# Down projection by two levels of Strassen's scheme in an S4-gated feed-forward kernel on one Trainium2 core

## The chip, the cores and the metric

The kernel runs on one core of one Trainium2 chip. A core has five engines with queues of their own: TensorE (PE; its weight loads are shown apart as PEld), VectorE (DVE), ScalarE (ACT), GpSimd (POOL) and SyncE (SP), which here only issues DMAs. TensorE writes to PSUM, which is split into eight banks of 128 partitions by 512 f32 numbers; the program names the banks x0, x1, w0, w1, y0, y1, aux0 and aux1. Everything is f32. The metric is the device time of one execution in microseconds; the median of several runs is compared. The lower, the better.

## The reference

The input u has 2 x 1024 rows of 512 numbers. The rows are normalised; a state-space model (S4) convolves each row causally along its 512 numbers; a gated feed-forward network with low-rank additions to each of its three weights gives a gate. Cut to what matters:

```python
xn = layernorm(u)                                   # along the last axis, 512
K  = s4_kernel(Lambda, p, q, B, Ct, step, 512)      # one convolution kernel for all rows
s  = causal_conv(xn, K) + D * xn                    # written with rfft/irfft of length 1024
h1 = lora_linear(xn, w1, A1, B1)                    # x @ w.T + 2 * (x @ a.T) @ b.T, 512 -> 1376
h3 = lora_linear(xn, w3, A3, B3)
f  = lora_linear(silu(h1) * h3, w2, A2, B2)         # 1376 -> 512
out = u + s * silu(f)
```

## The kernel before

The 2048 rows are four blocks of 512 tokens (TB); blocks 0 and 1 form half `sb` = 0, blocks 2 and 3 half 1. The first part of the program loads the rows, normalises and transposes them (channels on partitions) and adds the low-rank products to the weights in place (`merge`, DVE, out of PSUM).

**Up projections.** The hidden axis has ten chunks of 128 and a last one of 96 (`HID` 1376). The ten are handled as five pairs (`NPAIR`), each by two levels of Strassen's scheme in Winograd's form: an outer one over weight and token halves, with sums on DVE (`outer_weight_sums`, `inner_weight_sum`, `outer_token_sum`, `inner_token_sum`), and an inner one, so that a pair is seven chains (j = 1 to 7) of seven products (i = 1 to 7) of 128 x 128 by 128 x 512. Class `Chain` issues them: ACT copies PSUM to SBUF between products, DVE adds a snapshot to PSUM (`total`, line 780) and combines (`plus`, line 870), POOL does the combinations whose inputs are both in SBUF, ACT the SiLU and POOL the product (`Gate`, line 837), which SP stores to `g_dram` (`store_g`).

The order on every engine is written out by hand: `at(place, what)` puts a step into a heap, and the loop that pops it emits the instructions in order of place. A place is one product; chain n of pair c begins at place 7 (2 + 7c + n), and `PLACES` says where its seven products stand after that. Engines take their own queue in that order and wait by semaphores; a product waits for its bank, so a late DVE or ACT step holds up PE. The last pair begins at place `t0` = 210 and its last product stands at 265. Between these places stand the loading and merging of the down weight (`load_w2`, `merge_down`), the down projection's weight sums (`second_weights`, line 1221) and the first loads of the gates (`load_g`).

**Down projection.** Eight units of 128 tokens of two blocks (256 rows each) run one after another (the first four two by two). A unit is one level of the scheme: seven products, each summed over five chunk pairs, and four of them over the last chunk too, of 128 x 128 by 128 x 256 (function `unit`, lines 1316 to 1415; the matmuls are line 756 in `product`). The sums over the gates are made on DVE for two units at a time (`group_piece`, line 1179). The S4 kernel is made meanwhile, some steps at a time (`s4_resolvent`, `s4_roots`, `s4_matrix`, lines 554 to 747): vector steps on DVE and a few matmuls, with a result of five 128 x 128 blocks in the tile `conv`. Because the convolution can't start before that, the first four units set their gates aside in DRAM (`o_dram`), and each of the last four takes one back (`hold`, `take_back`) beside its own.

**Convolution and end.** `conv_product` (line 930 for its matmuls) makes the convolution of 128 rows by a Toeplitz matrix in 128 x 128 blocks: eight matmuls of 128 columns with sums of the transposed tokens (`block_sums`, DVE). `result` adds the shared part (line 1310, DVE), multiplies by the gate (line 1312, DVE), adds the row (line 1313, POOL) and stores it.

Of the kernel before, what the change touches and what calls it, by code (L numbers as in the profile page):

```python
# [12 lines left out]
F32 = mybir.dt.float32  # L13
# [4 lines left out]
P = 128  # L18
# [51 lines left out]
def exp_neg(nc, pool, x, times):  # L70

    magic = 1.5 * 2.0**23
    n = pool.tile([P, 1], F32, tag="ex_n", name="ex_n")
    nx = pool.tile([P, 1], F32, tag="ex_x", name="ex_x")
    r = pool.tile([P, 1], F32, tag="ex_r", name="ex_r")
    p = pool.tile([P, 1], F32, tag="ex_p", name="ex_p")
    two_n = pool.tile([P, 1], I32, tag="ex_2n", name="ex_2n")
# [16 lines left out]
    for k in range(6, -1, -1):  # L94
        nc.vector.tensor_scalar(p, p, r, 1.0 / math.factorial(k), ALU.mult, ALU.add)
        yield
    nc.vector.tensor_scalar(two_n, n, 127.0, 2.0**23, ALU.add, ALU.mult)
    yield
    out = pool.tile([P, 1], F32, tag="ex_out", name="ex_out")
    nc.vector.scalar_tensor_tensor(  # L100
        out, p, times, two_n.bitcast(F32), ALU.mult, ALU.mult
    )
# [5 lines left out]
def s4_gated_ffn(  # L108
# [70 lines left out]
    g_dram = dram.tile([NSB * NJ, P, NHC, 2, JW], F32, name="g_dram")  # L179

    b12_dram = dram.tile([P, NSB, 2, TB], F32, name="b12_dram")
    i12_dram = dram.tile([P, 3, TB], F32, name="i12_dram")

    UNITS, HOLD = 2 * NSB * NJ, NSB * NJ
    o_dram = dram.tile([HOLD, 2, P, DIM], F32, name="o_dram")
# [8 lines left out]
    xr = xpool.tile([P, 3, NSB, 2, TB], F32, name="xr")  # L194
    tin = ctx.enter_context(ExitStack())
# [5 lines left out]
    xt = upool.tile([P, 4, NSB, 2, TB], F32, name="xt")  # L201
# [128 lines left out]
    def spill():  # L330
        for sb in range(NSB):
            nc.sync.dma_start(out=b12_dram[:, sb], in_=b12[sb])
        nc.sync.dma_start(out=i12_dram, in_=xr[:, :, 1, 0, :])
# [165 lines left out]

    def load_w2_factors():  # L500
        lora_tiles(0)
        for g in range(4):
            load_lora(nc.sync, g, b2T, a2, 3 * P * g, min(3 * P * (g + 1), HID))
# [14 lines left out]
    def merge_down(i):  # L518

        made = []  # L520
        groups = [g for g in range(4) if i + 3 * g < NHC]
        ps = [bank("y", True), bank("w", True), *(aux() for _ in groups[2:])]
        for g, to in zip(groups, ps):
            lo = (i + 3 * g) * P
            fc = CHUNK_AT.index(lo)
            rows = P if fc < LAST else LASTR
            d, h = lora_factors(g, lo, rows)
            to = to[:rows, :]
            nc.tensor.matmul(to, lhsT=h, rhs=d, start=True, stop=True)  # L529
            made.append((w2_chunk(fc), to))  # L530
        for m, when in zip(made, (1.15, 2.3, 4.3, 4.4) if i < 2 else (1.15, 1.9, 2.6)):
            after(when, lambda m=m: merge(*m))
# [4 lines left out]
    def s4_tile(shape, name):  # L537
        return work.tile(shape, F32, name=name, bufs=1)

    def s4_loads():  # L540
        par = s4["par"] = s4_tile([P, 10], "par")
        nc.sync.dma_start(out=par, in_=s4_par)
        vc = s4["vc"] = s4_tile([NST, 2, 2, NST], "vc")
        for half in range(2):
            nc.sync.dma_start(out=vc[:, :, half, :], in_=vcT)
        bp_sb = s4["bp"] = s4_tile([NST, 1], "bp_sb")
        nc.sync.dma_start(out=bp_sb, in_=bp)
        hcol = s4["hcol"] = s4_tile([P, 4, NDC], "hcol")
        nc.sync.dma_start(out=hcol, in_=half_col)
        s4["trig"] = s4_room().rearrange("p (a l) -> p a l", a=3)  # L550
        nc.sync.dma_start(
            out=s4["trig"][:, :2].rearrange("p a l -> p (a l)"),
            in_=half_row.to_broadcast([P, 2 * DIM]),
        )
# [5 lines left out]
    def s4_room():  # L560
        return room["w"][:, 5 * DIM :]

    def s4_resolvent():
# [3 lines left out]
        par, trig = s4["par"], s4["trig"]  # L567
        cos, sin, im = (trig[:, i, :] for i in range(3))
        lam_r, lam_i = par[:, 0:1], par[:, 1:2]
        two_over_step = yield from exp_neg(nc, work, par[:, 8:9], 2.0)  # L570
        den = const.tile([P, DIM], F32, tag="lo_d", name="den")
# [16 lines left out]
        res = den  # L588
        nc.vector.tensor_tensor(res[:NST, :], re[:NST, :], den[:NST, :], mult)
        yield  # L590
        nc.vector.tensor_tensor(res[NST:, :], im[NST:, :], den[NST:, :], mult)
        yield


        pb = aux()
        for c in range(2):
            nc.tensor.matmul(
                pb[:, c : c + 1],
                lhsT=s4["vc"][:, c, :, :].rearrange("m h n -> m (h n)"),
                rhs=s4["bp"],  # L600
                start=True,
                stop=True,
            )
        yield from pause(3)
        y = s4_tile([P, 2, 2], "y")
        nc.vector.tensor_copy(y[:, :, 0], pb[:, 0:2])
        yield
        nc.vector.tensor_copy(y[:, :, 1], par[:, 6:8])
        yield

        v = s4_tile([P, 2, 2, 2], "v4")
        tmp = s4_tile([P, 2], "vtmp")
        for i in range(2):
            xr_, xi = par[:, 2 + 2 * i : 3 + 2 * i], par[:, 3 + 2 * i : 4 + 2 * i]
            nc.vector.tensor_scalar(tmp, y[:, 1, :], xi, None, mult)
            yield
            nc.vector.scalar_tensor_tensor(v[:, i, :, 0], y[:, 0, :], xr_, tmp, mult, add)
            yield
            nc.vector.tensor_scalar(tmp, y[:, 0, :], xi, None, mult)
            yield  # L620
            nc.vector.scalar_tensor_tensor(v[:, i, :, 1], y[:, 1, :], xr_, tmp, mult, sub)
            yield
        v4 = v.rearrange("p a b c -> p (a b) c")
        wv = s4_tile([P, 4, 2], "wv")
        nc.vector.tensor_copy(wv[:NST], v4[:NST])
        yield
        nc.vector.tensor_scalar(wv[NST:, :, 0], v4[NST:, :, 1], -1.0, None, mult)
        yield
        nc.vector.tensor_copy(wv[NST:, :, 1], v4[NST:, :, 0])
        yield  # L630
        s4["res"], s4["wv"] = res, wv
        yield from pause(8)

    def s4_roots():

        hcol = s4["hcol"]
        edft = s4["edft"] = s4_room().rearrange("p (a c j) -> p a c j", a=3, c=NDC)
        nc.sync.dma_start(out=edft[:, :2], in_=dft)
# [10 lines left out]
        k = s4_tile([P, NDC, 8], "k")  # L649
# [3 lines left out]
        cos, sin, cos_l, sin_l = (hcol[:, i, :] for i in range(4))  # L653

        def op(name, a, b, o):
            t = s4_tile([P, NDC], name)
            nc.vector.tensor_tensor(t, a, b, o)
            yield
            return t

        mul = mult
        dr = yield from op("dr", k11r, cos, mul)
        nc.vector.tensor_scalar(dr, dr, 1.0, None, add)
        yield
        di = yield from op("di", k11i, cos, mul)
        nr = yield from op("nr", k10r, cos, mul)
        ni = yield from op("ni", k10i, cos, mul)
        d2 = yield from op("d2", (yield from op("t0", dr, dr, mul)), (yield from op("t1", di, di, mul)), add)
        nc.vector.reciprocal(d2, d2)
        yield  # L670
        qr = yield from op("qr", (yield from op("t2", nr, dr, mul)), (yield from op("t3", ni, di, mul)), add)
        qi = yield from op("qi", (yield from op("t4", ni, dr, mul)), (yield from op("t5", nr, di, mul)), sub)
        nc.vector.tensor_tensor(qr, qr, d2, mul)
        yield
        nc.vector.tensor_tensor(qi, qi, d2, mul)
        yield
        mr = yield from op("mr", (yield from op("t6", k01r, qr, mul)), (yield from op("t7", k01i, qi, mul)), sub)
        mi = yield from op("mi", (yield from op("t8", k01r, qi, mul)), (yield from op("t9", k01i, qr, mul)), add)
        er = yield from op("er", k00r, mr, sub)
        ei = yield from op("ei", k00i, mi, sub)  # L680
        ar = yield from op("ar", (yield from op("u0", er, cos_l, mul)), (yield from op("u1", ei, sin_l, mul)), sub)
        ai = yield from op("ai", (yield from op("u2", er, sin_l, mul)), (yield from op("u3_", ei, cos_l, mul)), add)

        z = (edft[:, 2], room["zi"].rearrange("p (c j) -> p c j", c=NDC))
        for lc in range(NDC):
            e_r, e_i = edft[:, 0, lc, :], edft[:, 1, lc, :]
            a_r, a_i = ar[:, lc : lc + 1], ai[:, lc : lc + 1]
            for i, (f, g, o) in enumerate(((a_i, a_r, add), (a_r, a_i, sub))):
                tz = conv[:, DIM:]
                nc.vector.tensor_scalar(tz, e_i, f, None, mul)  # L690
                yield
                nc.vector.scalar_tensor_tensor(z[i][:, lc, :], e_r, g, tz, mul, o)
                yield
        s4["z"] = z
        yield from pause(8)

    def s4_matrix():
# [23 lines left out]
        f = s4["res"]  # L721
# [19 lines left out]
        k2s = s4["k2s"]  # L741
        both = conv[:, : 2 * P].rearrange("p (n t) -> p n t", n=2)
# [175 lines left out]

    def conv_product(lhs, x01, x12, sb, tok, tag):

# [391 lines left out]
    def unit(u, read, held=None, wait=False):  # L1316
# [8 lines left out]
        if u >= HOLD:  # L1325
            pl.load_in()
# [268 lines left out]
```

## Time and profile before

Three runs took 443.93, 442.70 and 442.58 us, median 442.7. The profiled execution has a span of 441.0 us from its first to its last instruction; the runs shown give no other time for that execution, so the median stands 1.7 us above the span.

| | busy, us | share of the span | instructions |
|---|---|---|---|
| PE | 434.3 | 98% | 1704 |
| PEld | 269.1 | 61% | 1704 |
| DVE | 317.6 | 72% | 536 |
| ACT | 144.3 | 33% | 296 |
| POOL | 207.9 | 47% | 156 |

An f32 matmul and its weight load are two records each in this table. DMA queues take 36.3% of sixteen engines' span and move 53.61 MB. The mean granted TensorE clock is 0.998. The first matmul of the down projection starts at 269.0 us of the span.

### The profile page before, as it was taken

How to read it: one execution, taken by the hardware profiler on the slowest of the kernel's cores; microseconds unless marked ns; L12 is line 12 of the kernel's file. 1: busy time of each engine (PE TensorE's matmuls, PEld its weight loads, DVE VectorE, ACT ScalarE, POOL GpSimd, SP SyncE). 2: the span in 40 equal slices, each digit the busy share in tenths (PEclk: the TensorE clock that was granted, in tenths of full speed). 3: DMA queues.
4: the chain of work that ended last, by engine and by line, in shares of the span. 5: the costliest groups of instructions: out<-in, count | busy, mean ns of one | idle time of the engine just before them, and what ended most of it. 6: DMA issues, size and time to landing. Idle time of an engine off the chain costs nothing.

```text
span 441.0 us, 5158 instructions
## 1 busy us (share of the span) xinstructions
PE 434.3 (98%) x1704; PEld 269.1 (61%) x1704; DVE 317.6 (72%) x536; ACT 144.3 (33%) x296; POOL 207.9 (47%) x156
## 2 busy tenths in 40 slices
PE   7999999999999999999999999999999999999996
PEld 7645334344444444444443446888898999999996
DVE  5899999954974687469745796979786885653234
ACT  2777242453255324532453242211101212212221
POOL 1416468895689368946894468400000122222221
PEclk9999999999999999999999999999999999999999
DMA  8931304025102500250035526395901832422211
GB/s 242 364 83 44 124 0 149 10 84 159 36 24 80 159 24 25 88 170 25 25 129 206 162 94 214 94 364 189 344 33 71 296 129 95 144 97 95 77 67 48
DMA packets 35467, 53.61 MB, mean 122 GB/s; under 512 B 4689, under 2 KB 21521, under 8 KB 35313
## 3 DMA queue, kind: packets, MB, share of 16 engines
q1 hardware_dynamic: 35088, 52.69, 36.3%
q10 hardware_dynamic: 352, 0.60, 0.4%
q8 instruction: 13, 0.21, 0.2%
q14 instruction: 14, 0.11, 0.1%
HBM read 33.88 MB, written 19.40 MB: 121 GB/s over the span
## 4 chain that ended last, share of the span: by engine, by line
PE 86%; DVE 7%; DMA 2%; ACT 2%; issue 1%; POOL 0%; SPq 0%; DVEq 0%; ACTq 0%; POOLq 0%
PE x L756 43%; PE y L756 22%; PE w L756 11%; PE aux L930 4%; PE w L930 2%; DMA s<-in_x_dram 1%; DVE xt L328 1%; DVE s L453 1%; DVE w L441 1%; DMA w<-in_w1T_dram 1%; PE y L529 1%; PE aux L711 1%; DVE t_in L343 1%; ACT c L254 1%; DVE aux L1310 1%
## 5 line engine op out<-in xcount | busy, mean ns | idle before, releaser
L1313 POOL TENSOR_TENSOR o<-o,xin 128x512 f32<-128x512 f32 (+1 forms) x17 | 23.3, 1369 | 133.0 <-DVE o L1312 133.0
L837 POOL TENSOR_TENSOR s<-c,s 128x512 f32<-128x512 f32 (+1 forms) x44 | 63.2, 1442 | 17.6 <-ACT c L829 12.4
L776 ACT COPY s<-x 128x512 f32<-128x512 f32 (+1 forms) x54 | 31.5, 584 | 84.5 <-PE x L756 84.4
L756 PE MATMUL x<-t_in,s 128*128 128x512 f32 (+1 forms) x148 | 55.4, 501 | 0.0
L870 POOL TENSOR_TENSOR s<-ua_three,s 128x512 f32<-128x512 f32 x20 | 35.9, 1793 | 25.4 <-DVE s L780 25.4
L780 DVE TENSOR_TENSOR s<-s,y 128x512 f32<-128x512 f32 (+1 forms) x54 | 36.0, 679 | 15.7 <-PE y L756 10.6
L756 PEld LDWEIGHTS x<-t_in,s 128*128 128x128 f32 x148 | 26.6, 190 | 23.3 <-issue 11.7
L870 POOL TENSOR_TENSOR ua_three<-ua_three,s 128x512 f32<-128x512 f32 x20 | 30.6, 1529 | 13.8 <-DVE s L780 13.8
L756 PE MATMUL y<-t_in,s 128*128 128x256 f32 (+1 forms) x108 | 35.9, 459 | 0.1
L1335 ACT COPY z<-x 128x256 f32<-128x256 f32 x24 | 8.8, 371 | 70.5 <-PE x L756 70.4
L870 POOL TENSOR_TENSOR s<-u_three,s 128x512 f32<-128x512 f32 x20 | 29.4, 1474 | 1.8 <-ACT c L829 1.0
L1310 DVE TENSOR_TENSOR aux<-aux,m 128x384 f32<-128x384 f32 x32 | 18.1, 565 | 15.8 <-PE aux L930 14.3
L829 ACT ACTIVATE c<-c 128x512 f32<-128x512 f32 x40 | 25.2, 632 | 12.9 <-DVE c L870 12.9
L756 PEld LDWEIGHTS y<-t_in,s 128*128 128x128 f32 x108 | 20.1, 190 | 11.6 <-issue 8.1
L794 ACT COPY w<-x 128x512 f32<-128x512 f32 (+1 forms) x37 | 21.1, 570 | 11.6 <-PE x L756 11.5
L870 POOL TENSOR_TENSOR u_three<-ua_three,u_three 128x512 f32<-128x512 f32 x10 | 15.6, 1556 | 13.4 <-DVE u_three L780 13.3
L756 PE MATMUL x<-t_in,w 128*128 128x512 f32 x40 | 21.0, 605 | 0.0
L756 PE MATMUL x<-xt,w 128*128 128x512 f32 x40 | 20.7, 598 | 0.0
L756 PE MATMUL x<-xr,w 128*128 128x512 f32 x40 | 20.6, 614 | 0.0
L756 PE MATMUL x<-xr,s 128*128 128x512 f32 x40 | 20.5, 614 | 0.0
L756 PE MATMUL x<-xt,s 128*128 128x512 f32 x40 | 20.4, 592 | 0.0
L756 PE MATMUL y<-xt,w 128*128 128x512 f32 x40 | 19.8, 592 | 0.0
(302 smaller groups left out, 908.7 us busy)
## 6 DMA issues: line engine op xcount, KB each, us to landing
g_dram<-s SPq DMA_DIRECT2D x40, 256.0 KB, 2.1
g<-g_dram SPq DMA_DIRECT2D x10, 512.0 KB, 5.8
xin<-in_x_dram SPq DMA_DIRECT2D x16, 256.0 KB, 2.7
out_dram<-o SPq DMA_DIRECT2D x14, 256.0 KB, 2.0
t_in<-g_dram SPq DMA_DIRECT2D x6, 512.0 KB, 4.1
w<-in_w1T_dram SPq DMA_DIRECT2D x10, 256.0 KB, 3.6
w<-in_w3T_dram SPq DMA_DIRECT2D x10, 256.0 KB, 4.9
t_in<-in_x_dram SPq DMA_DIRECT2D x8, 256.0 KB, 5.7
```

The lines of the kernel that those rows point to most:

```text
L254: nc.scalar.activation(value("c"), x_in[b][tt], AF.Copy, accum_out=sums_of_x[b][:, 0, tt : tt + 1])
L756: nc.tensor.matmul(ps[:, cols], lhsT=lhsT, rhs=rhs if parts == 1 else rhs[:, cols], start=first and i == 0 and part == 0, stop=i == len(pa ...
L776: nc.scalar.copy(t, self.x)
L780: nc.vector.tensor_tensor(t, t, self.y, add)
L794: nc.scalar.copy(self.w, self.x)
L829: nc.scalar.activation(c, c if src is None else src, AF.Silu)
L837: nc.gpsimd.tensor_tensor(g, act, g, mult)
L870: (nc.vector if o < 20 else nc.gpsimd).tensor_tensor(to, a, b, add)
L930: nc.tensor.matmul(to[:, n * P : (n + 1) * P], lhsT=x_, rhs=by, start=start, stop=True, skip_group_check=True,)
L1310: nc.vector.tensor_tensor(y[:, P:], y[:, P:], m[:, n * P : (n + 3) * P], add)
L1313: (nc.vector if last else nc.gpsimd).tensor_tensor(o, o, self.xin[h][:, cols], add)
L1335: nc.scalar.copy(t, xb)
```

## The change

The diff has some 1,300 lines. It does this:

- **Down projection in two levels.** Four units of 512 tokens (128 of each block) take the place of the eight. A unit has seven outer chains (j) of seven inner blocks (n); each block is a 128 x 128 by 128 x 128 product over two chunk pairs (eight chunks in all). The fifth pair of chunks and the last 96 rows go through the inner level alone, into the four outer chains of `EXTRA`. All of it is issued by `Unit.chain` and `down_product`.
- **Sums.** Weight: three more outer matrices on DVE and one in place (`weight_outer`), and seven inner sets (`weight_inner`). Gates: four outer sums of 1024 columns per unit, on POOL but for one (`g_outer`), and seven inner sets of four sums of 256 columns on DVE (`g_inner`), made ahead into a ring of nine places. The fifth pair: `rest_sums`, the first on DVE, the later ones on POOL.
- **Results.** Partial results stay in two banks of x, w or y; ACT takes snapshots; `combine` makes the four quarters of a gate on DVE out of four sources.
- **S4** runs between places 64 and 193 of the up projections; no gate is set aside in DRAM. The transposed tokens go to `x_dram` (`spill`) and come back unit by unit (`load_conv`) into places that the up projections have left; their convolution sums are on POOL (`conv_sums`).
- **Order.** After the up projections the places are microseconds: `pe(n, what)` advances a clock by n x 0.2236, and the other steps stand at fixed distances from it. It is an order of emission only.
- The chunks that load and merge the down weight are dealt to the row groups anew (`W2_AT`); `xt` lives on to the end.

Cut to its core:

```diff
-    UNITS, HOLD = 2 * NSB * NJ, NSB * NJ
-    o_dram = dram.tile([HOLD, 2, P, DIM], F32, name="o_dram")
+    UNITS = NTT
+    g_dram = dram.tile([UNITS, P, NHC, NSB, 2, P], F32, name="g_dram")
+    x_dram = dram.tile([UNITS, P, NDC, NSB, 2, P], F32, name="x_dram")
...
+    def inner_sums(eng, m, i, left, fifth=None):
+        m00, m10, m01, m11 = m
+        s2, s3, s4_ = i
+        s5 = m01 if fifth is None else fifth
+        if left:
+            todo = ((s3, m00, m01, sub), (s2, m11, s3, sub), (s5, m01, m11, add))
+        else:
+            todo = ((s3, m11, m01, sub), (s2, s3, m00, add), (s5, m01, m00, sub))
+        for to, a, b, op in (*todo, (s4_, m10, s2, sub)):
+            eng.tensor_tensor(to, a, b, op)
...
+    EXTRA = {2: (0, 0), 3: (0, 1), 7: (1, 1), 4: (1, 2)}
+    def down_product(u, j, n, to, plain=True, rest=True):
+        pairs = []
+        if plain:
+            a = inner_operand(*gi[u, j], True, n)
+            b = inner_operand(quarters(wm[j]), wi[j], False, n)
+            pairs += [(a[:, g], b[:, g]) for g in range(2)]
+        if rest and j in EXTRA:
+            ...
+        product(part(to, n), pairs, plain and j in (1, 7) and n in (1, 5))
...
+    steps(first, 64.1, 0.3, 33)
+    steps(first, 75, 1.5, 3)
+    steps(first, 118, 1.8, 12)
+    steps(s4_roots(), 142, 0.45, 80)
+    steps(s4_matrix(), 184, 0.3, 30)
+    at(t0 + 36, s4_shared)
+    at(t0 + 21.5, lambda: load_g(0))
+    for n, name in enumerate((5, 6)):
+        at(t0 + 30.5 + 3.2 * n, lambda name=name: g_outer(nc.gpsimd, 0, name))
+    at(t0 + 27, down_weights)
+    for n, name in enumerate((7, 6, 5, 4)):
+        at(t0 + 27.1 + 1.5 * n, lambda name=name: weight_outer(nc.vector, name))
+    for n, j in enumerate((1, 2)):
+        at(t0 + 37 + 4 * n, lambda j=j: weight_inner(nc.vector, j))
+    at(t0 + 42.5, lambda: g_inner(nc.vector, 0, 1, room["w"][:, 30 * P :]))
...
+    at(-0.5, lambda: load_rest(0))
+    at(0.2, lambda: g_inner(nc.vector, 0, 2, fifth[2]))
+    for when, j in ((0.5, 6), (3.7, 5), (6.9, 7), (10.1, 3), (17.5, 4)):
+        at(when, lambda j=j: weight_inner(nc.vector, j))
+        at(when + 1.5, lambda j=j: g_inner(nc.vector, 0, j, fifth.get(j)))
+    at(3, lambda: g_outer(nc.gpsimd, 0, 3))
+    at(4.5, lambda: g_outer(nc.vector, 0, 7))
+    for n in range(4):
+        at(11 + 1.5 * n, lambda: next(rw, None))
+    at(15, lambda: rest_sums(nc.vector, 0))
...
+        if h == 0:
+            at(clock[0] - (7.2, 10.4)[s], lambda: conv_sums(nc.gpsimd, u, s))
...
+        at(b[1] + 0.1, lambda: load_g(u))
+        if u == 1:
+            t5, t6, t3 = 16, 21.5, 24.5
+            whens = 28.5, 30, 36.5, 38.5, 41, 43, 45
+        for t, name in ((t5, 5), (t5 + 2.7, 7), (t6, 6), (t3, 3)):
+            at(t, lambda name=name: g_outer(nc.gpsimd, u, name))
+        for j, when in zip(order, whens):
+            at(when, lambda j=j: g_inner(nc.vector, u, j))
...
+    U = units[0]
+    for j in (1, 2, 6, 5, 7, 3):
+        U.chain(j, rest=j not in EXTRA)
+    for j in (2, 3, 7):
+        U.chain(j, plain=False)
+    conv_slot()
+    U.chain(4)
+    conv_slot()
+    ahead(U, 1)
+    for u in range(1, UNITS):
+        U, final = units[u], u == UNITS - 1
+        for j in FINAL if final else ORDER:
+            U.chain(j)
+            if j in ((6, 7, 4, 2) if final else (6, 3, 7, 4)):
+                conv_slot()
+            if final and j == 2:
+                conv_slot("y")
+        if not final:
+            ahead(U, u + 1)
```

`ORDER` is (1, 6, 5, 3, 2, 7, 4), `FINAL` (1, 6, 5, 7, 4, 2, 3). The very last convolution (`conv_last`) is issued column block by column block, ten matmuls in place of eight, so that its results can be finished one after another.

## The prediction

> **What bounds the kernel now.** I read the head of the page first, then busy time by stretches, then the chain that ended last in order of time, then the order of VectorE and GpSimd at the change of stage.
>
> ```profile
> PE 434.3 (98%) x1704; PEld 269.1 (61%) x1704; DVE 317.6 (72%) x536; ACT 144.3 (33%) x296; POOL 207.9 (47%) x156
> ...
> PE 86%; DVE 7%; DMA 2%; ACT 2%; issue 1%; POOL 0%; SPq 0%; DVEq 0%; ACTq 0%; POOLq 0%
> ```
>
> TensorE is busy 98% of the span and carries 86% of the chain. Stretches (start:end, length, then PE, PEld, DVE, ACT, POOL busy, clock, DMA share, GB/s):
>
> ```profile
> 180.00:210.00 30.00, 30.00 (x83) 12.68 (x83) 18.99 (x27) 10.92 (x20) 18.96 (x15) 1.00 0.31 95
> ...
> 252.00:257.00 5.00, 5.00 (x13) 2.12 (x12) 4.97 (x8) 1.88 (x4) 0.46 (x1) 1.00 0.30 97
> ...
> 272.00:277.00 5.00, 5.00 (x24) 4.37 (x24) 4.05 (x3) 0.00 (x0) 4.84 (x4) 1.00 0.27 92
> ```
>
> PE has no gap in the up projections, at the change of stage, or in the down projections, and the clock is full, so any product taken out shortens the run, as long as no wait comes in. The change of stage is the narrow place: DVE 4.97 of 5 at 252, POOL 4.84 of 5 at 272. In the chain (start, length, what) a matmul counts as two records, with its weight loads hidden:
>
> ```profile
> 310.58 1.03 PE aux L641 x8
> ...
> 328.13 2.68 PE aux L711 x24
> ...
> 370.60 1.12 PE aux L930 x10
> 371.71 2.16 PE x L756 x10
> ```
>
> So 128 columns take 1.12/5 = 0.224 us and 256 columns 2.16/5 = 0.432 us. The first down matmul starts at 269.00, the last ends at 437.25 (matmul records of the timeline): 168.25 us without a gap.
>
> **TensorE, removed and added.** Before: 8 units of 39 products of 256 columns (7 times 5 chunks, 4 for the last 96 rows) = 312 x 0.432 = 134.8, 16 convolution products of 8 matmuls = 128 x 0.224 = 28.7, S4 products 0.53 + 1.03 + 2.68 = 4.2; in all 167.7, against 168.25 measured. After: in each unit 7 chains of 7 blocks of 2 chunks (98), 28 for the fifth pair of chunks, 16 for the last rows, 32 for the convolutions = 174; four units and 2 more in the last convolution give 698 x 0.224 = 156.4. That is -11.9. The S4 products (4.2) move to the up projections, where PE is 30.00 of 30.00 busy, so they cost what they cost now. **Net -7.7.**
>
> [...]
>
> **S4's vector steps.** Some 30 us of DVE leave the down stage (284.9 to 335.6) for 64 to 193 places of the up order, with 7 to 13 us of idle DVE in each 30 us. They queue ahead of the chains' additions, which free PE's banks. One group, 4.6 us after the S4 matrix, lies among the outer weight sums of the last pair (199 to 206), where DVE runs without a pause. Bounds 0 to 3; I take 0.5, as the stretch has caught up by 206.45.
>
> **The end of the up projections.** Out: two weight sums of 1024 columns and three small ones (1.23 + 1.22 + 1.18 + 0.90 + 0.56 = 5.1 as measured). In, on DVE: four of 1024 (4 x 1.22), one of 256, and three inner sets of four of 256 at 0.34 from start to start (12 x 0.34): 9.3 us, of 23 between 246 and 269. On POOL two outer sums of 1024 (from 0.725 at 256 and 1.27 at 512 columns: estimate 2.36 each), which fall into its idle 5.8 us before 256.54, once load_g (on SP behind the gates' stores) has landed. The third weight set is queued ahead of the additions that release the y bank for the fourth chain's last product; in the trace that addition ends about 0.9 us before PE needs it. Without blocking DVE comes 1 to 2 us late; if every sum waits for a POOL operation, 5. Bounds 0 to 6; I take 1.
>
> **How DVE and POOL share.** A sum with both inputs in SBUF is stretched by a POOL operation, one that reads PSUM isn't (0.68 everywhere). Timeline, first DVE, then POOL (start, duration):
>
> ```profile
> 276.01 1.75 DVE L1179 TENSOR_TENSOR s<-room,s 128x512 f32<-128x512 f32 x1
> 277.68 2.28 DVE L1221 TENSOR_TENSOR w_a<-w_a 128x1024 f32<-128x1024 f32 x1
> 279.89 1.49 DVE L1221 TENSOR_TENSOR w_b<-w_b 128x256 f32<-128x256 f32 x1
> ...
> 277.17 1.71 POOL L870 TENSOR_TENSOR s<-ua_three,s 128x512 f32<-128x512 f32 x1
> 278.96 2.13 POOL L837 TENSOR_TENSOR s<-c,s 128x512 f32<-128x512 f32 x1
> ```
>
> Here they alternate strictly: the sum at 279.89 ends 0.29 after the POOL operation does. But elsewhere DVE keeps its turn:
>
> ```profile
> 48.53 1.28 DVE L328 TENSOR_TENSOR xt<-b,xr 128x512 f32<-128x512 f32 x2
> 49.73 1.28 DVE L328 TENSOR_TENSOR xt<-xr,xt 128x512 f32<-128x512 f32 x2
> 50.94 1.74 DVE L341 TENSOR_TENSOR t_in<-xr 128x1536 f32<-128x1536 f32 x1
> ...
> 48.69 5.12 POOL L870 TENSOR_TENSOR s<-ua_three,s 128x512 f32<-128x512 f32 x1 [6.04 <-DVE s L780]
> ```
>
> Five sums without a break ran undisturbed while POOL waited 4 us. [...]
>
> **The first unit.** PE runs six chains of 14 products (3.14 us each), so DVE must make two inner sets (8 x 0.34 = 2.7 us) per chain. By the third chain's third block (7.2 us after the start) ten sums must be done; they begin 0.65 after the last up product: 4.1 us if DVE keeps its turn, 3 us to spare. The next three chains need 24 sums and one of 1024, 9.3 us for 9.4 of PE; no slack is added there. If POOL's operations come between, 9 us late. The last gates, the load of the fifth pair and what stands behind it on SP also end here (second rival). Bounds 0 to 12; I take 2.5.
>
> **Units 1 to 3.** Per unit of 174 x 0.224 = 39.0 us, DVE: 28 inner sums (9.5), totals out of PSUM 2 x (0.57 + 0.68), combinations 4 x 1.2, convolution additions 8 x 0.58, products with the gate 4 x 0.61: 24 us. POOL: 4 outer sums (9.4), 4 + 10 of 256 columns (10.2), 4 of 512 (5.1): 24.7. The part that excludes the other is 24.7 + 9.5 + 2.4 = 36.6 of 39.0, close, but the sums are due a unit later and the banks have 1.3 to 3 us to spare. Bounds 0 to 6; I take 0.5. Covers: without these two engines free for a unit ahead, each late us is a PE us. DMA at 36% of the span changes little: 5.5 MB each way of set-aside gates and tokens goes, 4 MB each way comes.
>
> **Tail.** Now 437.25 to 437.94 + 0.29 on DVE. After: no SiLU (0.28) in it, but the additions for the last four column blocks all stand on DVE. -0.3 to +0.9; +0.3.
>
> **Sum.** The median is 442.7; the profiled span 441.0 lies 1.7 below it, and I keep that distance. -7.7 + 0.5 + 1 + 2.5 + 0.5 + 0.3 = -2.9: span 438.1, time **439.8**.
>
> **Rivals.**
> (1) Slower: DVE and POOL take turns at the start of the down stage. At the end of the up projections POOL has six operations left (270.25 to 281.09) and an outer sum. Six turns of 1.27 + 0.34, one of 2.36 + 0.34 and three free sums put the tenth sum at 14 us instead of 7.2: 7 us of PE, 2 more from the next unit's outer sums, 5 before the stage begins. 442.7 - 7.7 + 14 + 1.5 (the rest) = 450.5. For it: 272 to 281 above. Against: 48.5 to 52.7. It decides once these stalls pass 7 us in all.
> (2) No difference: the data chain. POOL's last gate ended 12.1 us after the first down matmul; store 2.1, issue 0.4, load 5.8 (DMA issues), sums 1.4: 21.8, needed at 19.5, so 2.3 late. Behind it on SP, load_g for unit 1 (3.2 to issue, about 6 to land, 23.8), two outer sums (4.7), then the five convolution sums (3.6): 32.1, needed at 28.5, 3.6 late. 442.7 - 7.7 + 5.9 + 1.3 = 442.2.
> (3) All hidden: 442.7 - 7.7 - 0.3 = 434.7.
>
> **How the numbers follow.** A measurement of this kernel tells 0.3% (1.3 us) from no change. Forecast 0.42, (1) 0.36, (2) 0.14, (3) 0.08. Faster: the forecast, (3) and an edge of (2), 0.50; within 0.3%: most of (2), 0.12; slower: (1) and the rest, 0.38. The range runs from 435.0 to 452.0; the forecast's own from 436.5 to 441.4.
>
> **What would show it.** Right: about 156 us from first to last down matmul, PE 30 of 30 in the up stretches, S4 products between 98 and 205 us, DVE sums of 0.42 in the first unit. Wrong: PE below 9 tenths around 255 to 300, DVE sums of 256 columns at 1 us and more there (1), PE waiting for the convolution's tokens or the fifth pair's sums (2), or more than 0.23 us per 128-column product.

## The result and the profile after

The changed kernel takes **507.2 us** (median of 4 runs, 506.0 to 509.1) against 442.6 before: a ratio of 1.147, 95% interval 1.143 to 1.150. It is slower by 65 us, outside the predicted range. The profiled run took 507.7 us with a span of 505.9.

From the page of the changed kernel: busy times; then the digits of VectorE, GpSimd and TensorE's granted clock over 40 slices of 12.6 us; then the chain that ended last.

```profile
PE 450.7 (89%) x2208; PEld 290.5 (57%) x2208; DVE 420.4 (83%) x690; ACT 148.1 (29%) x292; POOL 282.6 (56%) x224
...
DVE  6899999978788999478548999999999967974554
...
POOL 2344598836794664347936876822553469334432
PEclk9999999989999996999999997799899599979999
...
DVE 43%; PE 39%; issue 6%; DMA 5%; POOL 5%; ACT 2%; SPq 0%; DVEq 0%; POOLq 0%; ACTq 0%
```

Before, TensorE carried 86% of this chain and VectorE 7%; now VectorE carries more than TensorE. VectorE is at nine tenths or more in ten slices in a row (the 23rd, from 278 us on, to the 32nd), and the clock, full before, falls in seven slices. Stretches (bounds, length, PE, PEld, DVE, ACT, POOL busy, clock, DMA share, GB/s) show where:

```profile
85.00:108.00 23.00, 18.59 (x50) 7.29 (x52) 22.20 (x47) 8.64 (x15) 16.55 (x12) 1.00 0.39 109
...
300.00:340.00 40.00, 25.88 (x184) 24.43 (x183) 39.59 (x54) 3.44 (x7) 25.46 (x17) 0.83 0.41 126
...
380.00:405.00 25.00, 15.24 (x104) 13.90 (x103) 24.35 (x47) 2.13 (x6) 9.39 (x8) 0.74 0.22 71
405.00:440.00 35.00, 35.00 (x313) 35.00 (x312) 27.12 (x40) 7.07 (x17) 21.70 (x18) 0.99 0.36 112
```

In the three stretches where TensorE falls far short, VectorE is full (22.20 of 23, 39.59 of 40, 24.35 of 25). Where VectorE has room (405 to 440), TensorE does 313 matmul records in 35.00 us, two to a product: 0.224 us each, as predicted.

The excess of span, 505.9 - 441.0 = 64.9 us, adds up from the trace. Idle gaps of TensorE longer than 0.15 us: 48.7 against 1.3, so +47.4. Busy time of TensorE: 450.7, where 434.3 - 7.7 = 426.6 were due, so +24.1. Most of it comes from seven spans at half clock (granted clock 0.50, 3.4 to 13.7 us each, 51 us in all; before had none until its last 2 us) that begin within or shortly after a gap: 17 of the 51 us are themselves gaps, and the other 34 at half speed lose 17 (an estimate from these two numbers). The cause of the remaining 7 stays open. Tail from the last matmul: +1.1. Less work: -7.7. The gaps by place: 12.0 at 95 to 108 and 178 to 199, 5.4 at 261 to 298, 13.8 in the first unit, 16.5 in units 1 to 3. One of them, 1.3 us at 261, has another cause than a full VectorE, which was itself waiting for a load (in brackets its idle time and what ended it):

```profile
261.64 0.69 DVE L388 SCALAR_TENSOR_TENSOR w_a<-y,w_a 128x512 f32<-128x512 f32 x1 [3.89 <-DMA w_a<-in_w2T_dram]
```

The start of the down stage, first VectorE, then GpSimd (start, duration):

```profile
299.88 1.35 DVE L1158 TENSOR_TENSOR room<-xt 128x256 f32<-128x256 f32 x1
301.26 1.38 DVE L1158 TENSOR_TENSOR room<-xt,room 128x256 f32<-128x256 f32 x1
302.56 1.48 DVE L1158 TENSOR_TENSOR snap<-xt 128x256 f32<-128x256 f32 x1
...
309.59 2.56 DVE L1158 TENSOR_TENSOR t_in<-t_in,t_in 128x256 f32<-128x256 f32 x1
```

```profile
300.91 1.45 POOL L881 TENSOR_TENSOR ua_three<-ua_three,s 128x512 f32<-128x512 f32 x1
302.44 1.33 POOL L881 TENSOR_TENSOR s<-u_three,s 128x512 f32<-128x512 f32 x1
...
309.35 2.52 POOL L1218 TENSOR_TENSOR xr<-xt,xr 128x1024 f32<-128x1024 f32 x1
```

A VectorE sum of 256 columns, 0.42 alone, lasts about as long as the GpSimd instruction beside it: 1.4 beside 512 columns, 2.56 beside an outer sum of 1024. The S4 steps suffer in the same way: of 17 sums of 4 columns, most take 0.15, the longest 1.24 (minimum/median/maximum in ns):

```profile
L663 DVE TENSOR_TENSOR conv<-conv x17: 148/156/1240, 172.2 to 183.9; 128x4 f32<-128x4 f32 x17
```

### The profile page after: what moved, and what is told of

It is laid out like the page before. It is cut to its first block, busy times and chain, and to the rows that moved or that the text cites. A ratio compares the mean times of both kernels' runs of the same rounds, so it can differ in the third digit from the quotient of the medians.

```text
span 505.9 us, 6437 instructions
## 1 busy us (share of the span) xinstructions
PE 450.7 (89%) x2208; PEld 290.5 (57%) x2208; DVE 420.4 (83%) x690; ACT 148.1 (29%) x292; POOL 282.6 (56%) x224
## 4 chain that ended last, share of the span: by engine, by line
DVE 43%; PE 39%; issue 6%; DMA 5%; POOL 5%; ACT 2%; SPq 0%; DVEq 0%; POOLq 0%; ACTq 0%
PE x L769 17%; PE y L769 12%; DVE room L1158 7%; DVE t_in L1158 4%; PE w L769 4%; PE aux L1382 3%; DVE gi L1158 3%; DVE s L448 2%; DVE s L793 2%; POOL s L881 2%; DMA w_a<-in_w2T_dram 2%; DVE conv L663 2%; DVE c L881 1%; DVE xr L1158 1%; DVE aux L1406 1%
## 5 line engine op out<-in xcount | busy, mean ns | idle before, releaser
L1412 POOL TENSOR_TENSOR o<-o,xin 128x512 f32<-128x512 f32 (+1 forms) x16 | 19.7, 1233 | 87.8 <-DVE o L1411 47.6
L769 PE MATMUL x<-t_in,s 128*128 128x512 f32 x80 | 40.5, 615 | 0.0
L1382 PE MATMUL aux<-conv,xr 128*128 128x128 f32 x168 | 23.8, 288 | 8.1 <-POOL xr L1365 4.1
L1365 POOL TENSOR_TENSOR xr<-xr 128x256 f32<-128x256 f32 (+1 forms) x40 | 30.1, 770 | 1.5 <-DMA xr<-x_dram 0.2
L769 PE MATMUL y<-t_in,xt 128*128 128x128 f32 x128 | 22.4, 305 | 6.0 <-DVE snap L1520 6.0
L1317 ACT ACTIVATE o<-o 128x512 f32<-128x512 f32 x16 | 10.1, 633 | 59.7 <-DVE o L1332 50.4
L769 PEld LDWEIGHTS x<-t_in,s 128*128 128x128 f32 x80 | 14.3, 193 | 21.7 <-issue 12.6
L1382 PEld LDWEIGHTS aux<-conv,xr 128*128 128x128 f32 x168 | 21.3, 199 | 9.4 <-POOL xr L1365 5.2
L769 PEld LDWEIGHTS y<-t_in,xt 128*128 128x128 f32 x128 | 19.5, 218 | 6.5 <-DVE snap L1520 6.5
L769 PE MATMUL y<-xt,s 128*128 128x512 f32 x40 | 20.0, 597 | 2.2 <-DVE s L793 2.2
```

Source lines behind the costliest of these rows:

```text
L769: nc.tensor.matmul(ps[:, cols], lhsT=lhsT, rhs=rhs if parts == 1 else rhs[:, cols], start=first and i == 0 and part == 0, stop=i == len(pa ...
L1365: eng.tensor_tensor(to, a, b, op)
L1382: nc.tensor.matmul(to[:, n * P : (n + 1) * P], lhsT=x_, rhs=by, start=start, stop=True, skip_group_check=True,)
L1412: (eng or nc.gpsimd).tensor_tensor(o, o, rows_in[u, s, h][:, cols], add)
```

## The experiments

Theory (called turns, or conflict): a VectorE instruction that reads two tensors in SBUF waits until the running GpSimd instruction is over, so VectorE gets late and TensorE stands idle. Rival (load): VectorE simply has too much to do, whatever GpSimd does. A third question is whether the half clock costs time by itself. Ratios are against the kernel before, with 95% intervals.

**1. GpSimd's work narrowed** to a few columns, with the results left incomplete: in the up projections, in the down stage, and in both. VectorE's and TensorE's instructions stay.

```
-  (nc.vector if o < 20 else nc.gpsimd).tensor_tensor(to, a, b, add)
+  nc.vector as before; nc.gpsimd.tensor_tensor(to[:, :8], a[:, :8], b[:, :8], add)
-  nc.gpsimd.tensor_tensor(g, act, g, mult)
+  nc.gpsimd.tensor_tensor(g[:, :8], act[:, :8], g[:, :8], mult)
   down stage: g_outer on [:, :, :2], conv_sums and the added input on [:, :8]
```

> Changed kernel, but GpSimd's sums and products of the up projections (the parts of results that it adds, and the gates' products) work on 8 of 512 columns; VectorE's and TensorE's instructions are the same, and the gates' products are left incomplete. Theory (turns): a VectorE instruction with two operands in SBUF waits until GpSimd's running instruction is over, so the small steps of the S4 matrix took 1.2 us each instead of 0.15 to 0.3, and the sums at the start of the down stage 1.4 instead of 0.42. Then TensorE's gaps at 95 to 108, 178 to 198 and 261 to 298 us (about 19 us) go, 6.8 us lost at half clock in the up stage go, and the first gap of the first unit (5.4 us and 3.4 of slow clock) goes: about 472 us (465 to 485), and the S4 steps of 4 columns take under 0.3 us. Rival (load): VectorE merely has too many instructions, whatever GpSimd does: 500 us or more, and the steps stay at 0.4 to 1.2 us.

> Changed kernel, but GpSimd's instructions of the down stage (outer sums of the gates, sums for the convolution, adding the input) work on 8 columns or 2 of 256, and only rest_sums stays whole; VectorE and TensorE do the same, those sums are left incomplete. Turns: the gaps of units 1 to 3 (16.5 us) and their time at half clock (12 us) go, and in the first unit the gap before the seventh chain and the one after it (about 9 with their slow clock): about 470 us (462 to 485); 256-column sums at 0.42 from about 312 us on. Load: 500 us or more.

> Changed kernel with both narrowings of GpSimd's work (up projections and down stage, the columns left out as there). Turns: all gaps over 2 us go and the clock stays at full speed, the time falls to the sum that TensorE's products give: about 440 us (434 to 446). Load: VectorE's instructions are all still there, 490 us or more. If it lands between 450 and 480, both have a part.

Measured: 474.0 us (1.072, 1.070 to 1.073), 466.9 (1.055, 1.054 to 1.057) and **434.5** (0.983, 0.981 to 0.984). All three lie where turns put them, though VectorE's 690 instructions are untouched. The same S4 sums with GpSimd narrow in the up projections:

```profile
L663 DVE TENSOR_TENSOR conv<-conv x17: 148/157/175, 163.3 to 171.6; 128x4 f32<-128x4 f32 x17
```

And the page with both narrowed, where TensorE's gaps sum to 1.8 us:

```profile
PE 425.6 (98%) x2208; PEld 277.9 (64%) x2208; DVE 335.2 (77%) x690; ACT 148.1 (34%) x292; POOL 80.7 (19%) x224
...
PEclk9999999999999999999999999999999999999999
```

VectorE's busy time falls from 420.4 to 335.2 with the same instructions: 85 us of it were there only beside GpSimd's work, by the theory waits for turns. The clock stays full (mean 0.999, 0.948 in the changed kernel): the slow clock of the changed kernel came with TensorE's idle time.

**2. The control.** The same narrowing of the kernel before:

> Kernel before with the same narrowing of GpSimd's work (its sums, the gates' products and the addition of the input on 8 columns, those left incomplete). If the kernel before loses nothing to turns, as its TensorE without gaps after 20 us says, it stays at 442 us (441 to 443), and 434.5 against it is the products' saving of 7.7. If it gains as much as 7 us, that saving is not shown.

Measured: 440.3 us (0.995, 0.993 to 0.996), 0.7 below what was expected at least.

```profile
PE 432.8 (99%) x1704; PEld 269.8 (62%) x1704; DVE 294.8 (67%) x536; ACT 144.5 (33%) x296; POOL 59.3 (14%) x156
```

So the kernel before loses some 2.5 us to GpSimd's work, and freed of it the change saves 5.7 us of time and 432.8 - 425.6 = 7.2 of TensorE's busy time. VectorE's busy time falls here too, from 317.6 to 294.8: the kernel before also spent 23 us on turns, but at places where VectorE had room, so they cost it little. The change made 85 of them, many at places where it had none.

**3. The S4 matrix left out** (the convolution's matrix is zeros):

```
-  at(42, s4_begin)
...
-  steps(s4_matrix(), 184, 0.3, 30)
+  nc.gpsimd.memset(conv, 0.0)
```

> Changed kernel with the making of the S4 matrix left out (its 5 loads, 140 or so VectorE steps, 27 products; the convolution's matrix is zeros), all else as it was. The part of the change that put these steps into the up projections is sized by it: 4.2 us of products, 12 us of gaps at 95 to 108 and 178 to 198 us, and 6.8 us lost at half clock after them: about 484 us (478 to 490) if the rest of the kernel is not touched by it; the gaps from 261 us on stay. If the forecast's pricing (0.5 us for the steps) had been right, it would be 502.

Measured: 484.1 us (1.093, 1.090 to 1.096), as expected. The trace has 99 VectorE instructions and 36 matmul records (18 products) fewer, not the 140 and 27 of the expectation. The steps in the up projections cost 23 us with their 4.2 us of products, 19 without; the forecast had 0.5. The gaps behind them are in sum as in the changed kernel (36 us).

**4. The conflict put into the kernel before.** GpSimd is given work that nobody waits for, as 30 sums of 512 columns, as 120 sums of 128, and as 52 instructions with one operand:

```
+  noise = lora["h"][:, :DIM].rearrange("p (a b) -> p a b", a=4)
+  same = ident.unsqueeze(1).broadcast_to([P, 4, P])
+  for _ in range(30):
+      nc.gpsimd.tensor_tensor(noise, same, same, add)
   or 120 times  tensor_tensor(noise[:, i % 4], ident, ident, add)
   or 52 times   tensor_scalar(noise, same, 1.0, None, mult)
```

> Kernel before with 30 more sums of 512 columns on GpSimd at the start of its down stage: they read the identity matrix and write a place that nobody reads, so no instruction of the computation waits for one. Turns: GpSimd is busy with them from about 281 to 325 us or later, VectorE's instructions there with two operands in SBUF, the small S4 steps among them, take 1.2 us or more each instead of 0.15 to 0.95, VectorE falls behind TensorE, and the kernel takes 455 us (448 to 465). Load: nothing is added to VectorE, and the time stays at 442.4 within 1.

Measured: 459.6 us (1.039, 1.037 to 1.040): 17 us for instructions with no tie to the computation. VectorE had no work added, so load is refuted as the only cause of such a loss. VectorE in the kernel before, then with the noise (start, duration):

```profile
284.30 0.68 DVE L1179 TENSOR_TENSOR s<-room,s 128x512 f32<-128x512 f32 x1
...
286.66 0.15 DVE L86 SCALAR_TENSOR_TENSOR ex_r<-ex_n,ex_x 128x1 f32<-128x1 f32 x1
...
287.23 0.21 DVE L95 TENSOR_SCALAR ex_p<-ex_p,ex_r 128x1 f32<-128x1 f32 x1
```

```profile
285.78 1.19 DVE L1179 TENSOR_TENSOR s<-room,s 128x512 f32<-128x512 f32 x1
...
288.88 0.99 DVE L86 SCALAR_TENSOR_TENSOR ex_r<-ex_n,ex_x 128x1 f32<-128x1 f32 x1
...
290.29 0.21 DVE L95 TENSOR_SCALAR ex_p<-ex_p,ex_r 128x1 f32<-128x1 f32 x1
```

A sum of 512 columns waits 0.5 us, an instruction on a single column with two tensors in SBUF waits 0.84, a scaling of a single column doesn't wait (all seven of line 95 take 0.21).

> Kernel before with the same idle work on GpSimd as in before_pool_noise, in 120 sums of 128 columns instead of 30 of 512, again waiting for nothing and awaited by nobody. In split_pool one 256-column sum of VectorE lasted 11.1 us while 28 such pieces ran on GpSimd at 0.42 us each, where all later ones took 0.56 to 0.67. Fair turns: a VectorE instruction waits for one piece at most, 0.3 us more each, and the kernel takes 446 us (443 to 451). Starving: pieces that follow one another without a wait keep VectorE out until they are all done (50 us): one VectorE instruction of tens of us, and 470 us or more.

Measured: 457.3 us (1.033, 1.031 to 1.035), between the two expectations. Most waits were short (0.69 became 0.88), but one was not, again with VectorE first and GpSimd second:

```profile
315.70 8.94 DVE L657 TENSOR_TENSOR dr<-k,hcol 128x4 f32<-128x4 f32 x1
```

```profile
313.79 13.29 POOL L1265 TENSOR_TENSOR lo_h<-ident 128x128 f32<-128x128 f32 x37
```

> Kernel before with 52 idle GpSimd instructions of 512 columns with one operand (multiply by 1.0) at the start of the down stage in place of the 30 sums of two. If what VectorE waits for is any running GpSimd instruction, the time is like before_pool_noise (455 to 460). If only GpSimd's instructions with two operands do it, 442.4 within 1.

Measured: 451.2 us (1.017, 1.015 to 1.020): half the loss, between the two expectations, with GpSimd busy on these instructions for twice as long (83 us against 40). An instruction with one operand holds VectorE up too, but for less (sums of 512 columns at 0.69 became 0.69 to 1.09).

**5. GpSimd's instructions cut into 128 columns**, from the last pair on, and in the down stage alone:

```
+  def pieces(to, a, b, op, n):
+      for i in range(0, to.shape[-1], n):
+          cols = slice(i, i + n)
+          nc.gpsimd.tensor_tensor(to[..., cols], a[..., cols], b[..., cols], op)
```

> Changed kernel, same results, with GpSimd's instructions of the last pair of the up projections and of the down stage cut into pieces of 128 columns (of 512, 1024 and 256). GpSimd's work in columns is the same, its instructions four to eight times as many, and its total time grows. Turns: a sum of VectorE waits for one piece (0.45 us) instead of one whole instruction (1.33 to 2.5), so a 256-column sum takes up to 0.9 instead of 1.4 to 2.6, and the gaps from 299 us on shrink by a third to a half: about 485 us (475 to 497). Load: VectorE's own work is the same, and GpSimd is later with everything: 507 or more.

Measured: 505.8 us (1.141, 1.137 to 1.146), a miss. VectorE and GpSimd at the start of the down stage:

```profile
298.79 11.14 DVE L1166 TENSOR_TENSOR room<-xt 128x256 f32<-128x256 f32 x1
...
311.64 0.67 DVE L1166 TENSOR_TENSOR t_in<-t_in 128x256 f32<-128x256 f32 x1
```

```profile
299.63 1.69 POOL L870 TENSOR_TENSOR s<-c,s 128x128 f32<-128x128 f32 x4
...
306.24 3.34 POOL L870 TENSOR_TENSOR s<-c,s 128x128 f32<-128x128 f32 x8
```

Contested sums of 256 columns take 0.67 instead of 1.4 to 2.6, as expected, but the first one waits while at least 24 pieces in a row go by (the 16 from 299.63 on and the eight from 306.24), and TensorE has one gap of 7.9 us there.

> Changed kernel, same results, with GpSimd's instructions cut into pieces of 128 columns in the down stage only (outer sums, convolution's sums, adding the input); the gates' products and sums of the up projections stay whole, so that the eight left over at 299 to 309 us hold VectorE up one by one as in the changed kernel. Turns: contested 256-column sums after 310 us take 0.56 to 0.67 instead of 1.4 to 2.6, the gap of 5.4 at 307 stays, those after it shrink by a third: about 497 us (491 to 503). Load: 507 or more.

Measured: 499.2 us (1.126, 1.122 to 1.130), as turns had it: the size of GpSimd's instructions matters. But in units 1 to 3 the convolution sums on GpSimd, now later, keep TensorE waiting mostly 1.4 to 1.8 us each instead of 0.9 to 1.2.

**6. Work moved between the two engines.** The S4 steps to GpSimd; GpSimd's down stage to VectorE:

```
-  nc.vector.<op>(...)   in exp_neg, s4_vectors, s4_resolvent, s4_roots, s4_matrix
+  nc.gpsimd.<op>(...)
```

```
-  g_outer(nc.gpsimd, ...), rest_sums(nc.gpsimd, u), conv_sums(nc.gpsimd, u, s)
+  g_outer(nc.vector, ...), rest_sums(nc.vector, u), conv_sums(nc.vector, u, s)
-  (eng or nc.gpsimd).tensor_tensor(o, o, rows_in...)
+  (eng or nc.vector).tensor_tensor(o, o, rows_in...)
```

> Changed kernel, same results, with the steps of the S4 matrix in the up projections on GpSimd (each multiply-and-add as two instructions; the copies out of PSUM on ScalarE, the reciprocals and two of the last sums stay on VectorE). GpSimd's own small instructions are short, so VectorE loses its turn for a short time only. Turns: TensorE's gaps at 95 to 108 and 178 to 198 us and the half clock after them go: about 488 us (484 to 495), near the kernel without S4 (484.1). If the place in the up projections is the cost, whichever engine does it: 500 or more.

Measured: 520.8 us (1.178, 1.175 to 1.181), slower than the change itself. The number falls on the side of "the place is the cost, whichever engine does it", but the trace gives a reason of its own. What SP's queue waited for (total, times, longest), and VectorE's instruction at the largest gap:

```profile
SPq L827 <- POOL s L854: 41.5, 5, 18.8
```

```profile
223.45 0.69 DVE L394 SCALAR_TENSOR_TENSOR w<-y,w 128x512 f32<-128x512 f32 x1 [16.79 <-DMA w<-in_w1T_dram]
```

GpSimd fell behind with the gates; SP, which stores them in order, waited up to 18.8 us for one; the next pair's weights, queued behind on SP, came late; TensorE stood 14.2 us. That GpSimd had no room itself was in neither expectation, so the run doesn't decide between them.

> Changed kernel, same results, with all of GpSimd's work of the down stage on VectorE: 14 sums of 1024 columns at 1.22, 38 of 256 or 128 at 0.42, 14 additions of 512 at 0.69, 9 rest sums, some 45 us. With GpSimd's instructions narrowed VectorE's instructions from 277 us on took 123 us, in the changed kernel 176 from 299 on. Turns: 123 and 45 are 168, about what is there to use, so the down stage is bound by VectorE's own work and the leftovers at its start: about 485 us (476 to 498), faster than the changed kernel though VectorE is given 45 us more. Load: VectorE's 176 become 220, 530 us or more.

Measured: 491.2 us (1.108, 1.106 to 1.110), inside what turns gave. VectorE does 85 instructions more, and is busy for as long as in the changed kernel (420.4):

```profile
PE 445.3 (91%) x2208; PEld 286.1 (58%) x2208; DVE 419.5 (86%) x775; ACT 147.9 (30%) x292; POOL 186.3 (38%) x139
```

**7. Half clock.** Products that wait for nothing, into the gaps of the first unit:

```
+  FILL = {(0, 6, 6, True): 21, (0, 7, 6, True): 18, (0, 2, 6, False): 10}
+  keep_warm(psum_aux, FILL.get((self.u, j, n, plain), 0), True)
```

> Changed kernel, same results, with 49 idle products of 128 columns into an unused bank of PSUM, put ahead of the three products of the first unit that wait longest for VectorE's sums (21 at 307.6 us, 18 at 321.4, 10 at 335.6: 4.7, 4.0 and 2.2 us of work in gaps of 5.4, 4.8 and 2.8). They wait for nothing. The question is whether the half clock costs anything by itself. If it follows from TensorE's idle time, the spans at half clock at 310 to 317 and 324 to 331 us go. If the half speed is then on the path, the kernel gains up to 6.8 us (to 500.5); if VectorE's sums set the pace of the first unit anyway, it gains 0 to 3 (504 to 507). If the clock has another cause, the spans stay.

Measured: 508.3 us (1.151, 1.146 to 1.155), no gain. The first unit in the changed kernel, then with the filling:

```profile
299.00:345.00 46.00, 31.81 (x233) 30.12 (x233) 44.97 (x68) 4.51 (x10) 26.46 (x18) 0.85 0.38 117
```

```profile
299.00:345.00 46.00, 40.05 (x329) 39.31 (x329) 44.86 (x69) 4.34 (x9) 26.10 (x17) 0.93 0.36 109
```

The clock rose from 0.85 to 0.93 and one of the two slow spans went; VectorE was at 45 of 46 us both times. So the half clock follows idle time in this case, and in the first unit it costs nothing that these runs show: TensorE would only wait longer for VectorE.

In the up projections it does cost time, and the traces show how much. After the same three gaps at 95 to 108 us, the changed kernel, down_pool_narrow, split_down and down_on_dve have a span of 3.4 us at half clock; warm_fill, split_pool and mend_down (below) have none, with the same code up to there. The changed kernel, then warm_fill:

```profile
108.00:114.00 6.00, 6.00 (x25) 2.73 (x18) 3.43 (x7) 1.12 (x2) 1.56 (x2) 0.72 0.08 24
```

```profile
108.00:114.00 6.00, 6.00 (x29) 2.80 (x22) 5.10 (x9) 1.12 (x2) 2.54 (x2) 1.00 0.05 17
```

From the end of the third gap to the start of the next one, near 178 us, TensorE works for 71.25 to 71.27 us in the four with the span and for 69.57 in each of the three without: 1.7 us, half of the span. What the half clock costs in units 1 to 3 stays open.

**8. Moves around the narrow places.** While the S4 steps run, from the end of the up projections on, and both:

```
-  (nc.vector if o < 20 else nc.gpsimd).tensor_tensor(to, a, b, add)
+  (nc.vector if o < 20 or on_vector() else nc.gpsimd).tensor_tensor(to, a, b, add)
   gates' product likewise; on_vector(): places 62 to 77 and 140 to 196, or from 240 on
   from 240 on also: g_outer(nc.vector, ...), conv_sums about 6 us earlier
```

> Changed kernel, same results, with GpSimd's sums and gates' products on VectorE while the small S4 steps run (about 85 to 105 and 168 to 210 us), elsewhere as it was. VectorE gets some 30 sums of 512 columns at 0.69 that took 1.27 and more on GpSimd. Conflict: the S4 steps take 0.15 to 0.3 us, the gaps at 95 to 108 and 178 to 198 (12 us) and their half clock (6.8) mostly go: about 491 us (486 to 498). Load: VectorE has 20 us more to do in the places where TensorE waits for it: 507 or more.

> Changed kernel, same results, with the gates' sums and products of the last fifth of the up projections and the 16 outer sums of the gates (1024 columns) on VectorE, and the convolution's sums, still on GpSimd, some 6 us earlier. Conflict: no GpSimd leftovers at 299 to 311 us, no sums of 2.5 us later: the gaps of the first unit go from 13 to about 6 us, those of units 1 to 3 from 16.5 to about 9, with half the time at slow clock: about 483 us (474 to 494). Load: VectorE's work grows by 25 us in a stage where it is busy 90 percent of the time: 507 or more.

> Changed kernel, same results, with both moves. Conflict: the gains add up: about 467 us (458 to 480), still slower than the kernel before, since VectorE's own work then fills the down stage. Load: 507 or more. Below 442 would need every gap gone, which the narrowed kernel reached (434.5) only without GpSimd's work.

Measured: 503.7 us (1.138, 1.131 to 1.144), 498.0 (1.125, 1.121 to 1.128) and 495.1 (1.117, 1.114 to 1.120). They gain 3.5, 9 and 12 us on the change where conflict put 16, 24 and 40: the sign is as it said (in mend_up the intervals still touch), the sizes are a miss. In mend_up the S4 sums are undisturbed, and yet TensorE's gaps are nearly the same (11.1 us at these places against 12.0):

```profile
L664 DVE TENSOR_TENSOR conv<-conv x17: 150/155/164, 171.5 to 183.1; 128x4 f32<-128x4 f32 x17
```

```profile
90.00:110.00 20.00, 15.46 (x48) 6.20 (x48) 18.89 (x48) 6.35 (x12) 5.53 (x4) 1.00 0.41 120
...
170.00:215.00 45.00, 38.33 (x108) 15.72 (x107) 40.93 (x98) 15.08 (x27) 0.00 (x0) 1.00 0.25 70
...
183.00:198.00 15.00, 9.27 (x20) 3.03 (x19) 14.54 (x38) 3.32 (x7) 0.00 (x0) 1.00 0.20 54
```

GpSimd does nothing between 170 and 215, no instruction waits for it, and where the gaps lie VectorE is full with the sums it was given (18.89 of 20, 14.54 of 15). So around the S4 steps conflict alone is not the cause: the work of both engines, which run one at a time over much of it, doesn't fit beside TensorE there, in the order in which it is issued. Our reading, which no run isolates: narrowing helped in full because it took the work away, and moving takes off only the part by which VectorE is quicker (0.69 against 1.27 us for 512 columns). No version with the whole work comes near the kernel before; the fastest is down_on_dve.

## Why the prediction was wrong

**TensorE's products: right.** -11.9 in the down stage: with GpSimd narrowed the down matmuls take 156.2 us from first to last (156.4 predicted), and TensorE's busy time falls by 7.2 (7.7). The row of 0.224 us was right too: 313 records in 35.00 us give the same 0.224 after the change. The 434.5 us of the run with GpSimd narrowed is also what the third rival, all hidden, gave (434.7), in part by luck, since the narrowing alone takes 2.5 us off the kernel before.

**S4's vector steps: the first failure.** Taken 0.5, bounds 0 to 3; measured 19. The step set 30 us of short instructions against idle VectorE time, with the durations of the place they came from. There GpSimd was idle. At the new place it is busy 16.55 of 23 us, and an instruction of 0.15 to 0.3 lasts up to 1.24 when it meets one of GpSimd's. The idle time was also less than the text had: not 7 to 13 us in each 30 but 5.1 between 150 and 180, where VectorE was busy for 24.91. That the waits are not the whole of it, mend_up shows: without them the gaps stay.

**The end of the up projections.** Taken 1, bounds 0 to 6, measured gaps 5.4. That is near the text's 5, "if every sum waits for a POOL operation", but not every sum waited (the set at 290 to 293.6 took 0.58, 1.37, 1.49 and 0.41), and 1.3 of the 5.4 is the load of the down weight at 261.

**How DVE and POOL share: the choice that failed.** The text had both rows, strict turns at 276 to 281 and VectorE keeping its turn at 48 to 53, and built the forecast on the second. The first was nearer: in the rows at 299.88 to 309.59 a VectorE sum of 1.35 to 2.56 us, 0.42 alone, ends about 0.28 after the GpSimd instruction beside it, and 85 us of VectorE's time went that way, 23 in the kernel before. The row at 48.53, where VectorE kept its turn, gave no rule; the waits of 8.94 and 11.14 us show the opposite, GpSimd keeping its turn for many instructions, which neither row had. The first rival did price turns, but only around the start of the down stage, and its 450.5 is still 57 us short.

**The first unit.** Taken 2.5, bounds 0 to 12; gaps 13.8. The first rival named this mechanism and put the tenth sum at 14 us; it was due at 7.2 and ended 13.6 after the first down product, so that TensorE waited 5.4. But the rival gave all that followed in this unit 2 us; there sums met outer sums at 2.4 to 2.6 us each (gaps of 4.8 and 2.8).

**Units 1 to 3.** Taken 0.5, bounds 0 to 6; gaps 16.5. The text had 36.6 of 39.0 us of mutually exclusive work per unit and called it close. With 94% of the time bespoken an instruction out of place can become a wait: in the second unit a convolution waits 4.0 us for VectorE and the next three for GpSimd's sums, 0.9 to 1.0 each.

**The clock** had no term. It fell to half with the gaps, which is some 17 of the 24 us by which TensorE's busy time is over what was due; the part in the up projections is already in the 19 of the S4 steps. **Tail:** +0.3 taken, 1.1 measured.

**The second rival** (loads and SP) put 5.9 us on the gates' data and the convolution's tokens; in the changed kernel the one gap that a load explains is the 1.3 us at 261, for the down weight. It is large only in s4_on_pool, when GpSimd was made late.

## What to carry to other kernels

Price a moved instruction by what runs beside it at its new place, not by the row of the old one: a step of 0.15 us lasted up to 1.24 where GpSimd was at work. Add up VectorE's and GpSimd's two-operand SBUF work as if it were one engine, stage by stage, and compare it with TensorE's time: here 36.6 of 39.0 us per unit was too close, and 16.5 us went in three units. Moving all sums of a stage to VectorE gained 16 us here, still far from the kernel before. When narrowing an engine's work heals everything, run also a version that moves the work, before the healing is put down to conflict alone.

## What was not expected of the hardware

GpSimd kept VectorE out for many instructions: 8.94 us (before_noise_pieces) and 11.14 us (split_pool) in rows of 128-column pieces without a wait between them, while beside other such pieces VectorE got its turn after 0.2 to 0.3 us. What decides it, the traces don't show. A VectorE scaling of two columns waited (1.19 us instead of 0.23), the scaling of a single column didn't (0.21). The clock's slow spans in the changed kernel last 3.4 us or a multiple of it (3.4, 6.8, 10.2, 13.7), and a gap of 2.4 us (at 359.1) is followed by one, a gap of 2.8 (at 335.6) isn't; after the same gaps at 95 to 108 us four traces have a span and three have none.
